# A four-layer graph network: two transposes per graph moved from TensorE to a round trip through HBM, and a new order of the work

## Chip, core and metric

One core of a Trainium2 chip runs the whole program in one launch. The metric is the device time of one execution in microseconds (us), as the median of several runs.

## What is computed

Sixteen graphs of 1024 nodes each have features x (1024 x 128) and a weighted symmetric-pattern adjacency matrix adj (1024 x 1024), all in 32-bit floats. Four layers follow one another, each of the form x = x + layer(relu(layernorm(x))):

```
# layer 0, three times (i = 0, 1, 2), relu between
h = h @ W_i + b_i;  nh = h / |h|
h = (adj * (nh @ nh.T)) @ h
# layer 1
y = relu(((1+eps)*h + h.T-aggregate over adj) @ W1 + b1) @ W2 + b2, masked by nodes
# layer 2
h = h @ W;  e = tanh(s1_i + s2_j);  softmax over the edges;  e @ h
# layer 3
h = x @ W.T + b;  e = (h@A) @ h.T, plus its transpose;  softmax where adj > 0
h' = relu((att * adj) @ h);  three gates from x and h';  o * tanh(sigmoid(i*h' + f*x))
```

## The kernel before

The kernel keeps one graph ("batch" in the code, b = 0 to 15) in SBUF while it goes through its layers. A feature matrix of 1024 x 128 is one tile of 128 partitions x 1024 elements: eight blocks of 128 nodes. The adjacency is worked through in eight rows of blocks, j = 0 to 7, and each row in two halves of 512 columns (HALVES).

No order of the work is written out by hand. The functions `layer0` to `layer3` only record operations in a `Plan`: each has an engine, a planned duration, the tiles that it reads and writes, and a function that emits the instructions. `Plan.order` then lists them: among the operations that could start now on an engine it takes the one with the lowest `rank`, and it gives out buffers within limits per kind of tile (`KINDS`: how many in all, and how many for graphs younger than the oldest one). So up to three graphs are in flight (`AHEAD`), and an engine's instructions of different graphs are interleaved. Each engine executes its list strictly in that order. DMAs are nearly all issued from SP's queue, which is in order too: a DMA that waits for its source holds up those behind it.

Before the change, `rank` is a deadline of the graph (one every 59 planned us), less the planned length of what still hangs on the operation, less a number from the table `LEADS`.

What the change touches:

- `layernorm` makes hn: statistics on VectorE (L700, L709, L711), the power -1/2 on GpSimd (L592), then half of the blocks scaled by VectorE (L728) and the other half by ScalarE with the relu in it (L735). `relu` (L756) is a ScalarE instruction for VectorE's half.
- `flipped` transposes a feature matrix on TensorE: eight 128x128 transposes by the identity in two groups of four (L599), each group into one PSUM bank, and two ScalarE evictions of 128x512 (L652), which do the relu where it is wanted. It is used for layer 0's first features (tile hT, from PSUM tile ps_hT), for h in each of layer 0's three steps (hTn), and in layers 2 and 3 (hnT from ps_hnT; h3T).
- `squares` is the other way to a transpose, and before the change nothing calls it. It writes the matrix to an HBM buffer (one DMA of 512 KB), reads it back in four DMAs of 128 KB in pieces of 32 elements, so that every 32x32 square lands in its transposed place, and turns all squares within themselves by one VectorE transpose of 128x1024. A DMA of the same shape is in use elsewhere: `Square.send` sends the blocks above the diagonal (L832, by_hbm<-above, 512 KB) through HBM and reads them back (L843, got<-by_hbm, 4 x 128 KB) for the squares of layers 0 and 3. The adjacency itself is loaded in squares and turned by VectorE (L939, L947).
- `layer0` uses `squares` for hT if the flag "D" is set and b > 1; `layer3` uses it for hnT if the flag "3" is set.
- After layer 2, the last accumulation (L863, acc<-h,e) is divided by its row sums (L1196 to L1204) and added to x (L674); then comes layer 3's layernorm.
- The first TensorE work on hT is `project` (L630, psP<-w,hT); on layer 3's hnT also L630 (psP<-w3e,hnT), and L640 (pg<-hnT,wg).

Of the kernel before, what the change touches and what calls it, by code (L numbers as in the profile page):

```python
# [11 lines left out]
AF = mybir.ActivationFunctionType  # L12
# [3 lines left out]
P = 128  # L16
N = 1024
NB = N // P
D = 128
# [26 lines left out]
class Op:  # L46
    def __init__(self, engine, us, fn, batch, port, lat):
        self.engine, self.us, self.fn, self.batch, self.port, self.lat = engine, us, fn, batch, port, lat
        self.preds, self.succs, self.after = set(), set(), set()
        self.new, self.bufs = [], []  # L50
        self.waits = 0
        self.tail, self.key = 0.0, None
        self.end = None


class Plan:
# [8 lines left out]
    def __init__(self, pools, kinds, deadline, ahead, window, leads):  # L65


        self.pools, self.kinds = pools, kinds
        self.deadline, self.ahead, self.window, self.leads = deadline, ahead, window, leads
        self.psum = {k for k, v in kinds.items() if v[0] == "bank"}  # L70
        self.ops = []
# [38 lines left out]
    def link(self):  # L110
# [23 lines left out]
        for o in reversed(self.ops):  # L134
            o.tail = o.us + max((s.tail + o.lat for s in o.succs), default=0.0)
            lead = self.leads.get(o.key + o.edge, self.leads.get(o.key, 0.0))
            o.rank = (self.deadline(o.batch) - o.tail - lead, o.seq)
# [87 lines left out]
def tile_adj_preln(  # L225
# [40 lines left out]
    FLAGS = set("CabcdkxhyzTGmrHWM")  # L266
# [61 lines left out]
    for load_it in first:  # L328
# [13 lines left out]
        "adjT": ("adjT", 16, 16), "adjL": ("adjL", 5, 5), "x": ("x", 3, 3), "w4": ("big", 9, 11),  # L342
        "chunk": ("big", 10, 4), "above": ("above", 2, 1), "got": ("got", 1, 1), "ps": ("bank", 8, 8),
        "acc": ("bank", 8, 6), "small": ("small", 8, 15), "row": ("row", 3, 2), "hbm": ("hbm", 3, 3),
        "hrow": ("hrow", 1, 2), "mask": ("mask", 5, 5), "dot": ("dot", 8, 6),
    }
    PERIOD, LAST, AHEAD, WINDOW = 59, 47, 2, 0.05

    LEADS = {
        "T DMA raw": 8063, "T PE raw": 0, "T ACT adjT": -100.5, "T DVE su": 407, "x DMA x": -299,  # L350
        "0 DVE st": -1917, "0 DVE mv": 384.5, "0 POOL rstd": -16.5, "0 DVE nb": 0.5, "0 DVE hn": -46.5,
        "0 ACT hn": -776, "0 PE ps": -292, "0 ACT hT": 79, "00 PE psP": 1440, "00 DVE h": -784,
        "00 PE ps": -672.5, "00 ACT hTn": 614, "00 ACT sq": -476, "00 DVE ss": 222.5, "00 POOL rn": 13,
        "00 PE sq": 10.5, "00 ACT above": 37, "00 DVE ew": 444, "00 PE acc0": -2418.5, "00 POOL params": 0,
        "00 DMA params": -366, "00 DVE params": 242, "00 PE params": 0, "00 ACT hT": 294.5, "01 PE psP": 195.5,
        "01 DVE h": 274.5, "01 PE ps": 22.5, "01 ACT hTn": -282.5, "01 ACT sq": -278, "01 DVE ss": -245,
        "01 POOL rn": 168.5, "01 PE sq": -205.5, "01 ACT above": -385.5, "01 DVE ew": 1895,
        "01 PE acc0": -206.5, "01 ACT hT": 248, "02 PE psP": 2916.5, "02 DVE h": 758, "02 PE ps": 31,
        "02 ACT hTn": -1183.5, "02 ACT sq": -620.5, "02 DVE ss": 22, "02 POOL rn": 75, "02 PE sq": 1500.5,
        "02 ACT above": -53, "02 DVE ew": -1, "02 PE acc0": -128.5, "02 DVE x": -282.5, "T DMA adjT": 69,  # L360
        "T DVE adjT": -537, "1 DVE st": -155, "1 DVE mv": 935.5, "1 POOL rstd": 141.5, "1 DVE nb": 917.5,
        "1 DVE hn": 519, "1 ACT hn": 0, "1 DVE x": 1302, "1 DMA adjL": -249, "1 DVE adjL": -959.5,
        "1 PE acc1": 121, "1 ACT g": -58.5, "1 PE py": -1925.5, "1 ACT y1": -654, "1 PE py2": -657.5,
        "2 DVE st": 2939, "2 DVE mv": 451.5, "2 POOL rstd": -7.5, "2 DVE nb": 458.5, "2 DVE hn": 103.5,
        "2 ACT hn": -1908.5, "2 PE ps": 207, "2 ACT hnT": -1905, "2 DVE alone": 776.5, "2 DVE x": -134,
        "2 PE psP": -2328.5, "2 ACT h": -84.5, "2 DVE hrow": -74, "2 PE pf": -2468, "2 ACT hfl": -232,
        "2 PE pt": -2412, "2 ACT sr": -23.5, "2 DMA sd": 272, "2 DMA s1": -44.5, "2 DVE h": 238.5,
        "2 ACT e2": -712, "2 DVE e2": 1.5, "2 PE acc2": -14.5, "2 DVE rden": -158.5, "3 DVE st": -169,
        "3 DVE mv": 49.5, "3 POOL rstd": -377.5, "3 DVE nb": -198, "3 DVE hn": -200.5, "3 ACT hn": -305,
        "3 PE ps": 733, "3 ACT hnT": 328.5, "3 PE pg": 105, "3 ACT gT": -285, "3 PE psP": 1188.5,  # L370
        "3 DVE h": -34.5, "3 ACT h3T": 171.5, "3 ACT mask": -341, "3 PE sq": 363.5, "3 ACT above": 296,
        "3 DVE e3": -798.5, "3 DVE top": -299.5, "3 ACT e3": 670.5, "3 DVE sum": -391, "3 ACT hs": 802,
        "3 PE acc3": -717, "3 ACT hpT": 0, "3 PE psN": 255.5, "3 ACT hp": 229, "3 DVE gate": -304.5,
        "3 ACT gate": 367.5, "3 POOL z": -81, "3 DVE z": -1115, "3 ACT z": -461, "3 DMA z": -361,
        "00 DVE above": -24.5, "00 DMA by": -55, "00 DMA got": 222, "01 DVE above": -5, "01 DMA by": 71,
        "01 DMA got": -599.5, "02 DVE above": 13, "02 DMA by": 225.5, "02 DMA got": 175, "3 DVE above": -234,
        "3 DMA by": 492, "3 DMA got": -1024.5, "3 DVE mask": -757, "3 POOL e3": 15, "3 POOL hp": -384.5,
        "2 PE p1": -264, "2 ACT s1": 222.5, "T DMA raw <0": -410.5, "T PE raw <0": -234,
        "T ACT adjT <0": -47.5, "T DVE su <0": 695, "x DMA x <0": -310.5, "0 DVE st <0": 245.5,
        "0 DVE mv <0": -814.5, "0 POOL rstd <0": -699, "0 DVE nb <0": 4.5, "0 DVE hn <0": -97.5,  # L380
        "0 ACT hn <0": -48, "0 PE ps <0": 50.5, "0 ACT hT <0": 14, "00 PE psP <0": 107, "00 DVE h <0": -116,
        "00 PE ps <0": -292, "00 ACT hTn <0": 127.5, "00 ACT sq <0": -40, "00 DVE ss <0": 80.5,
        "00 POOL rn <0": 581, "00 PE sq <0": -14, "00 ACT above <0": 604, "00 DVE ew <0": -578,
        "00 PE acc0 <0": -283, "00 POOL params <0": -577, "00 DMA params <0": -90.5, "00 DVE params <0": -71,
        "00 PE params <0": 27, "00 ACT hT <0": -242.5, "01 PE psP <0": 141.5, "01 DVE h <0": -33,
        "01 PE ps <0": -283, "01 ACT hTn <0": -13, "01 ACT sq <0": -152.5, "01 DVE ss <0": 216.5,
        "01 POOL rn <0": 15, "01 PE sq <0": 910.5, "01 ACT above <0": -520.5, "01 DVE ew <0": 130,
        "01 PE acc0 <0": 29, "01 ACT hT <0": -137, "02 PE psP <0": -86, "02 DVE h <0": 136,
        "02 PE ps <0": -146, "02 ACT hTn <0": -22.5, "02 ACT sq <0": 335, "02 DVE ss <0": -136.5,
        "02 POOL rn <0": 159.5, "02 PE sq <0": -157, "02 ACT above <0": 703, "02 DVE ew <0": 157,  # L390
        "02 PE acc0 <0": -197.5, "02 DVE x <0": -109, "T DMA adjT <1": 0, "T DVE adjT <1": -784.5,
        "T ACT adjT <1": 115, "1 DVE st <0": -232, "1 DVE mv <0": -95, "1 POOL rstd <0": -224,
        "1 DVE nb <0": -381.5, "1 DVE hn <0": 457.5, "1 ACT hn <0": 107.5, "1 DVE x <0": 63.5,
        "1 DMA adjL <0": -1413.5, "1 DVE adjL <0": -39, "1 PE acc1 <0": -15.5, "1 ACT g <0": 1108,
        "1 PE py <0": -156.5, "1 ACT y1 <0": 317.5, "1 PE py2 <0": -101, "2 DVE st <0": -262.5,
        "2 DVE mv <0": -681.5, "2 POOL rstd <0": -18, "2 DVE nb <0": 115.5, "2 DVE hn <0": -192,
        "2 ACT hn <0": 439, "2 PE ps <0": 115.5, "2 ACT hnT <0": -20.5, "2 DVE alone <0": 130,
        "2 DVE x <0": 88.5, "2 PE psP <0": 210, "2 ACT h <0": -87.5, "2 DVE hrow <0": -270, "2 PE pf <0": 410,
        "2 ACT hfl <0": -958, "2 PE pt <0": 89.5, "2 ACT sr <0": -58, "2 DMA sd <0": -787, "2 DMA s1 <0": -107,
        "2 DVE h <0": -143.5, "2 ACT e2 <0": 40, "2 DVE e2 <0": -511, "2 PE acc2 <0": 12.5,  # L400
        "2 DVE rden <0": -46.5, "3 DVE st <0": -67.5, "3 DVE mv <0": 182, "3 POOL rstd <0": 198.5,
# [96 lines left out]
    def op(engine, us, reads, writes, fn, port=False, lat=None):  # L498
        o = plan.op(engine, us, reads, writes, fn, now[0], port, lat)
        t = (list(writes) + list(reads))[0]  # L500
        o.key = f"{now[1]} {engine} {(t[0] if isinstance(t, tuple) else t).name.split('_')[0]}"

        o.edge = f" <{now[0]}" if now[0] < 2 else f" >{B - 1 - now[0]}" if now[0] > B - 3 else ""
        return o

    def pe(us, reads, writes, fn):
# [1039 lines left out]
```

## Time and profile before

| | |
|---|---|
| median of 3 runs | 2411.78 us (2411.68 to 2414.8) |
| the profiled execution | 2413.47 us, of which span 2411.7 us |
| mean granted TensorE clock | 0.996 |
| TensorE matmuls busy | 2384.0 us (99%), 11905 records |
| VectorE, ScalarE, GpSimd busy | 1985.5 (82%), 1474.7 (61%), 251.1 (10%) us |
| DMA | 271.31 MB, mean 112 GB/s |

How to read it: the span is from the first to the last instruction of the profiled execution. A matmul of 32-bit floats stands as two records in the trace, a transpose as one. Matmuls overlap in the pipeline, so a record's duration (275 ns for 128 columns) is longer than its cost; what one costs is the distance between the starts of neighbours that wait for nothing. "L852" is line 852 of the kernel. A line of a timeline has: start in us, length in us, engine, line, operation, out<-in, shapes, how many instructions were merged (x), and in brackets the idle time before them with what ended it.

### The profile page before, as it was taken

To read this page: it belongs to the slowest core of one execution; us is meant where nothing else is said; L and a number is where in the kernel's file an instruction comes from. 1 tells how busy PE (TensorE), PEld (TensorE's weight loads), DVE (VectorE), ACT (ScalarE), POOL (GpSimd) and SP (SyncE) were. 2 spreads that over 40 slices of the span, in tenths; PEclk is the share of its full clock that TensorE was granted. 3 is DMA by queue.
4 is the path that set the end of the run, shared out by engine and by line. 5 is a ranking of instruction groups with operands and counts; after the bars stand their busy time and mean duration, and the time that the engine had idled before them with its cause. 6 is when DMAs were issued, how large, how long until landed. Compare 5 with 4: busy or idle time off the path is not lost.

```text
span 2411.7 us, 35199 instructions
## 1 busy us (share of the span) xinstructions
PE 2384.0 (99%) x11905; PEld 1586.1 (66%) x11905; DVE 1985.5 (82%) x5529; ACT 1474.7 (61%) x2629; POOL 251.1 (10%) x168
## 2 busy tenths in 40 slices
PE   8999999999999999999999999999999999999988
PEld 5568576675766757576675766757667575765864
DVE  7658889887888988889888898878898787787767
ACT  7326756656675666666656566565756656654566
POOL 3100010110101010000100101101011100100012
PEclk9999999999999999999999999999999999999998
DMA  9232829457393683928748295573936738045100
GB/s 201 61 105 62 166 63 172 125 105 166 72 176 94 136 152 81 183 62 159 148 86 160 71 171 127 105 160 75 172 102 129 155 76 157 27 76 101 34 11 18
DMA packets 1103541, 271.31 MB, mean 112 GB/s; under 512 B 937224, under 2 KB 1084816, under 8 KB 1103360
## 3 DMA queue, kind: packets, MB, share of 16 engines
q1 hardware_dynamic: 1083200, 258.35, 53.7%
q10 hardware_dynamic: 19264, 9.70, 1.4%
q8 instruction: 94, 1.54, 0.3%
q0 software_dynamic: 896, 1.01, 0.2%
q14 instruction: 87, 0.71, 0.1%
HBM read 206.00 MB, written 62.98 MB: 112 GB/s over the span
## 4 chain that ended last, share of the span: by engine, by line
PE 95%; SPq 1%; DVE 1%; ACT 1%; DMA 1%; issue 0%; DVEq 0%
PE acc L852 35%; PE sq L790 20%; PE acc L863 18%; PE psP L630 6%; PE sq L800 4%; PE py L1081 2%; PE py L640 2%; PE ps_hTn L599 2%; PE psN L630 1%; PE ps_hnT L599 1%; PE pg L640 1%; SPq L939 1%; PE ps_h3T L599 1%; PE ps_hT L599 0%; ACT e L1175 0%; DVE ew L1019 0%
## 5 line engine op out<-in xcount | busy, mean ns | idle before, releaser
L1019 DVE SCALAR_TENSOR_TENSOR ew<-sq,rn,adjT 128x512 f32<-128x512 f32 x612 | 434.4, 739 | 86.8 <-ACT above L822 53.6
L852 PE MATMUL acc<-ew,h 128*128 128x512 f32 x1024 | 478.1, 593 | 1.5 <-DVE ew L1019 1.5
L790 PE MATMUL sq<-hTn 128*128 128x512 f32 (+3 forms) x1152 | 432.2, 489 | 0.1
L822 ACT COPY above<-sq 128x384 f32<-128x384 f32 (+3 forms) x432 | 167.7, 393 | 415.9 <-PE sq L800 225.1
L790 PEld LDWEIGHTS sq<-hTn 128*128 128x128 f32 x1152 | 196.9, 190 | 148.3 <-issue 95.7
L852 PEld LDWEIGHTS acc<-ew,h 128*128 128x128 f32 x1024 | 180.4, 190 | 166.2 <-issue 137.3
L863 PEld LDWEIGHTS acc<-h,ew 128*128 128x128 f32 x2048 | 241.0, 192 | 19.9 <-issue 11.4
L863 PE MATMUL acc<-h,ew 128*128 128x128 f32 x2048 | 249.6, 275 | 0.0
L852 PE MATMUL acc<-e,hs 128*128 128x512 f32 x512 | 238.3, 594 | 0.0
L863 PEld LDWEIGHTS acc<-h,e 128*128 128x128 f32 x2048 | 231.8, 192 | 8.4 <-PE acc L852 3.5
L863 PE MATMUL acc<-h,e 128*128 128x129 f32 x2048 | 233.3, 275 | 0.1
L852 PE MATMUL acc<-adjL,hn 128*128 128x512 f32 x512 | 232.8, 592 | 0.0
L592 POOL TENSOR_TENSOR rstd<-ve,mhalf 128x8 f32<-128x8 f32 x64 | 108.9, 1702 | 1054.4 <-DVE ve L711 989.1
L800 PEld LDWEIGHTS sq<-ident,above 128*128 128x128 f32 x960 | 126.1, 141 | 113.1 <-issue 89.7
L950 ACT ACTIVATE adjT<-adjT 128x1024 f32<-128x1024 f32 x120 | 126.6, 1055 | 101.0 <-DVE adjT L947 99.2
L800 PE MATMUL sq<-ident,above 128*128 128x128 f32 x960 | 175.2, 273 | 0.0
L1183 DVE SCALAR_TENSOR_TENSOR e<-adjT,e 128x512 f32<-128x512 f32 x256 | 159.6, 682 | 11.9 <-ACT e L1179 11.9
L1313 DVE TENSOR_TENSOR e<-e,adjT 128x512 f32<-128x512 f32 x248 | 162.0, 682 | 3.8 <-ACT e L1304 3.7
L852 PEld LDWEIGHTS acc<-adjL,hn 128*128 128x128 f32 x512 | 93.5, 190 | 101.2 <-issue 87.7
L812 DVE STREAM_TRANSPOSE above<-sq 128x512 f32<-128x512 f32 x208 | 145.0, 706 | 15.8 <-PE sq L790 14.7
L947 DVE STREAM_TRANSPOSE adjT<-adjT 128x1024 f32<-128x1024 f32 x120 | 144.5, 1221 | 13.9 <-DMA adjT<-in_adj_dram 13.2
L1272 DVE CUSTOM_DVE_ANT_0 e<-mask,sq 128x512 f32<-128x512 int8 x204 | 135.5, 676 | 20.1 <-ACT above L822 12.0
(161 smaller groups left out, 3672.2 us busy)
## 6 DMA issues: line engine op xcount, KB each, us to landing
adjL<-in_adj_dram SPq DMA_DIRECT2D x128, 512.0 KB, 5.0
adjT<-in_adj_dram SPq DMA_DIRECT2D x480, 128.0 KB, 3.9
by_hbm<-above SPq DMA_DIRECT2D x104, 512.0 KB, 4.0
got<-by_hbm SPq DMA_DIRECT2D x416, 128.0 KB, 3.0
s<-sd SPq DMA_DIRECT2D x15, 512.0 KB, 3.5
out_dram<-z ACTq DMA_DIRECT2D x15, 512.0 KB, 3.3
x<-in_x_dram SPq DMA_DIRECT2D x13, 512.0 KB
raw<-in_adj_dram SPq DMA_DIRECT2D x8, 512.0 KB, 8.0
```

Of the source, the lines that this page charges most:

```text
L630: nc.tensor.matmul(dst.t[:, (c - lo) * n : (c - lo + 1) * n], cols(srcT.t, c), w, start=True, stop=True)
L790: lambda: nc.tensor.matmul(dst.t[:, (first - lo) * P :], cols(leftT.t, j), span(rightT.t, first, hi), start=True, stop=True),
L800: nc.tensor.transpose(cols(dst.t, r), cols(above.t, p), ident)
L812: lambda: nc.vector.transpose(span(above.t, p, p + 4), read.t),
L822: lambda: nc.scalar.copy(span(above.t, p, p + hi - first), read.t[:, (first - lo) * P :]),
L852: lambda s=s, lo=lo, hi=hi: nc.tensor.matmul(acc[s].t, cols(h.t, at, w), span(ew.t, lo, hi), start=(j == 0), stop=(j == NB - 1)),
L863: nc.tensor.matmul(a.t[:, (c - lo) * n : (c - lo + 1) * n], cols(ew.t, c), h.t[:, at * w : at * w + n], start=(j == 0 and c == lo), stop=( ...
L947: dve(V(N), [t], [t], lambda t=t: nc.vector.transpose(t.t, t.t), True)
L1019: lambda view=view, ew=ew, rn=rn, j=j, lo=lo, hi=hi: nc.vector.scalar_tensor_tensor(by_block(span(ew.t, lo, hi), D, 4), view(), rn.t[:, j ...
L1183: lambda e=e, j=j, lo=lo, hi=hi: nc.vector.scalar_tensor_tensor(span(e.t, lo, hi), span(aT[j].t, lo, hi), 0.0, span(e.t, lo, hi), op0=ALU. ...
L1272: lambda e=e, view=view, mask=mask, peak=peak, s=s, lo=lo, hi=hi: nc.vector.tensor_tensor_reduce(by_block(span(e.t, lo, hi), D, 4), by_blo ...
L1313: lambda e=e, j=j, lo=lo, hi=hi: nc.vector.tensor_mul(span(e.t, lo, hi), span(e.t, lo, hi), span(aT[j].t, lo, hi)),
```

## The change

Four things:

1. The flags "D" and "3" are set, so `squares` takes the place of `flipped` for layer 0's first features in graphs 2 to 15 (14 graphs) and, with an added condition 0 < b < 14, for layer 3's hn in graphs 1 to 13 (13 graphs). `squares` gets a width parameter, used only in code behind flags that are not set ("4", "6").
2. `rank` is now the time at which the operation is due: graph number times PERIOD plus an entry of the table TIMES, which has one number for each single operation of a kind (LEADS had one for all of a kind). Tables for the first two and the last two graphs stand apart, as they did.
3. PERIOD is 144.89 in place of 59. It is a number of the planner.
4. The limits in KINDS change for most kinds; the pools themselves are as before.

```diff
-            o.rank = (self.deadline(o.batch) - o.tail - lead, o.seq)
...
-    FLAGS = set("CabcdkxhyzTGmrHWM")
+    FLAGS = set("CabcdkxhyzTGmrHWMD3")
...
-        ... "w4": ("big", 9, 11),
-        "chunk": ("big", 10, 4), "above": ("above", 2, 1), ... "ps": ("bank", 8, 8),
-        "acc": ("bank", 8, 6), "small": ("small", 8, 15), "row": ("row", 3, 2), "hbm": ("hbm", 3, 3),
-        "hrow": ("hrow", 1, 2), "mask": ("mask", 5, 5), "dot": ("dot", 8, 6),
+        ... "w4": ("big", 9, 6),
+        "chunk": ("big", 9, 8), "above": ("above", 2, 2), ... "ps": ("bank", 6, 7),
+        "acc": ("bank", 6, 8), "small": ("small", 9, 12), "row": ("row", 2, 4), "hbm": ("hbm", 3, 2),
+        "hrow": ("hrow", 2, 1), "mask": ("mask", 5, 5), "dot": ("dot", 10, 8),
...
-    PERIOD, LAST, AHEAD, WINDOW = 59, 47, 2, 0.05
+    PERIOD, AHEAD, WINDOW = 144.89, 2, 0.05
...
+    TIMES = {
+        "T DMA raw <0": [45.7, -38, -16.15, 49.25, 9.05, 10.9, 32.75, 4.4],
...
+        o.nth = counts.get((o.batch, o.key), 0)
+        counts[o.batch, o.key] = o.nth + 1
+        due = TIMES[o.key + o.edge if o.key + o.edge in TIMES else o.key][o.nth]
+        o.rank = (o.batch * PERIOD + due, o.seq)
...
-        if "3" in FLAGS and b < B - 2:
+        if "3" in FLAGS and 0 < b < B - 2:
             relu(hn)
             hnT = squares(hn, f"hnT_{k}")
         else:
             hnT = flipped(hn, f"hnT_{k}", AF.Relu)
             relu(hn)
```

The function that takes the place of `flipped`, as it stands before (the change only adds a width to the read):

```
    def squares(src, name):
        d = Buf("hbm", [N, D], f"d_{name}")
        op("DMA", 0.7, [src], [d], lambda: nc.sync.dma_start(..., by_block(src.t)), lat=2.2)
        dst = w4(name)
        def fetch():
            v = d.t.rearrange("(a i) (g j) -> g i a j", i=SQ, j=SQ)
            for g in range(P // SQ):
                nc.sync.dma_start(dst.t[g * SQ : (g + 1) * SQ, 0:N].rearrange(...), v[g])
        op("DMA", 3.6, [d], [dst], fetch, lat=2.4)
        dve(V(N), [dst], [dst], lambda: nc.vector.transpose(dst.t[:, 0:N], dst.t[:, 0:N]), True)
        return dst
```

In the built program this is, against before: 216 TensorE transposes fewer; 27 VectorE transposes of 128x1024 more; 54 ScalarE evictions of 128x512 fewer and 14 relus of 128x512 more; 27 writes of 512 KB and 108 reads of 128 KB more on SP's queue. Everything else is there in the same number (some are merged or split by four or eight blocks), in another order.

## Prediction

> **What bounds the kernel now.** I read the page's busy line first, then stretches of one graph each, then the stretch between layer 2 and layer 3 of one graph on TensorE, and last the end of the span.
>
> ```profile
> PE 2384.0 (99%) x11905; PEld 1586.1 (66%) x11905; DVE 1985.5 (82%) x5529; ACT 1474.7 (61%) x2629; POOL 251.1 (10%) x168
> ```
>
> A busy TensorE alone proves little, so I take the distance between starts. Each group's usual distance (429 ns for a record of 512 columns, 112 ns for 128, 109 ns for a transpose), times its records, sums to 2361.6 us. The first matmul starts at 7.6 and the last group ends at 2400.9, so some 32 us in all lie in longer distances; 10.8 us follow the last matmul. The kernel is bound by how much TensorE is given to do.
>
> The stretches of busy time, here two of four periods that I read (us, then busy us of PE, PEld, DVE, ACT, POOL; granted clock; DMA share; GB/s):
>
> ```profile
> 904.10:1050.70 146.60, 146.60 (x728) 97.08 (x727) 125.46 (x349) 92.33 (x163) 13.70 (x8) 1.00 0.63 126
> 1050.70:1197.30 146.60, 146.60 (x728) 97.09 (x727) 125.46 (x349) 92.34 (x163) 13.70 (x8) 1.00 0.64 126
> ```
>
> They repeat to the digit. One graph's records at the usual distances come to 145.75 us, so only 0.87 us of a period is waiting. VectorE has 21 us free in each, ScalarE 54.
>
> TensorE's timeline between layer 2's last product of one graph and its layer 3:
>
> ```profile
> 1065.73 1.17 PE L863 MATMUL acc<-h,e 128*128 128x129 f32 x9
> ...
> 1077.28 0.60 PE L599 MATMUL ps_hT<-ident,hn 128*128 128x128 f32 x4
> 1077.72 2.84 PE L630 MATMUL psP<-w,hT 128*128 128x128 f32 x24
> 1080.40 1.04 PE L599 MATMUL ps_hnT<-ident,hn 128*128 128x128 f32 x8
> 1081.27 1.04 PE L599 MATMUL ps_hTn<-ident,h 128*128 128x128 f32 x8
> ```
>
> Layer 2 ends at 1066.90; the transposes of layer 3's hn start 13.5 us later and take 0.87 us for eight (1080.40 to 1081.27), 109 ns each. ScalarE's timeline says when hn was ready:
>
> ```profile
> 1078.46 1.64 ACT L735 ACTIVATE hn<-x,nb,rstd 128x128 f32<-128x128 f32 x4
> ```
>
> At 1080.10, 13.2 us after layer 2: hn comes just in time. That chain stays, and it decides whether a longer route to the transposed hn fits.
>
> [...]
> - [...] a transpose's record is 273 ns long, its cost 109 ns.
> - [...] The trace has VectorE's turn of 128x1024 at 1221 ns (L947), TensorE's eight at 0.87 us plus two evictions of 0.593.
> [...]
>
> **The change part by part.**
>
> *TensorE gives up 216 transposes* (8 for each of 14 layer-0 and 13 layer-3 turns): 216 x 0.109 = 23.6 us. All of it lies on the bounding engine. In the middle, 16 x 0.109 = 1.74 us per period.
>
> *ScalarE* gives up 54 evictions (L652, 0.595) and gains 14 relus (L756, 0.62): -23.5 us of an engine with 54 us free per period; nothing on the path.
>
> *VectorE* gains 27 x 1.22 = 33 us, two turns a period: 125.5 + 2.4 of then 144.9 us, 88%. Hidden behind TensorE's matmuls while 17 us a period are free; without that cover 33 us.
>
> *DMA:* 27 writes and 108 reads, 28 MB, on SP's queue, which moved 258 MB. Share 0.64 to about 0.70. By itself hidden.
>
> *The new waits.* The route for layer 3 is hn, relu of VectorE's half, write, read, VectorE's turn. Its time I take from the like-shaped DMAs of `Square.send`, SP's timeline:
>
> ```profile
> 1044.44 0.37 SPq L832 DMA_DIRECT2D by_hbm<-above  x1
> 1047.45 2.26 SPq L843 DMA_DIRECT2D got<-by_hbm  x4
> ```
>
> The write releases the first read after 3.0 us; the last read is issued some 4.6 us after the write and lands 2.2 to 3.3 us later by that tile's view: about 7.5 us in all. Among other traffic it is longer: 1090.39 to 1093.78 and 3.14 us of issuing, plus the median 3.0 to landing, 9.5; the page's median 4.0 for the write makes it 10.1. In the stretch that matters, before, DMA rests:
>
> ```profile
> 1080.40:1090.30 9.90, 9.90 (x59) 7.19 (x58) 6.97 (x16) 6.59 (x13) 1.64 (x1) 1.00 0.00 1
> ```
>
> and in the built order SP has nothing between layer 0's read and this write. So I take 7.5, upper end 10.1. From layer 2's end: 13.2 + 0.6 relu + 0.2 issue + 7.5 + 1.2 turn + 0.2 = 22.9 us. In the built order of the changed kernel, TensorE has between graph 7's last layer-2 product and its first use of hnT 14 matmuls of 512 columns (0.858), 2 of 384, 2 of 256, 30 of 128 and 28 transposes: 23.9 us, where before it was 13.7 to the transposes. Margin 1.0 us, so no stall; at 10.1, 1.6 us late. Queued behind VectorE's waiting turn are layer 0's multiplications (ew, L1019) of the next graph, and TensorE's accumulations wait for those.
>
> Layer 0's route starts from x, loaded long ahead; the write goes out before layer 3's in SP's order and its turn stands on VectorE between nb and other work, so only DMA time above some 10 us would show. Cost 0; upper end 1 us a turn.
>
> *The new order elsewhere.* 0.87 us of waiting per period may go or double: -10 to +10 us over 12 periods; I take 0. At the start the same transposes of the raw adjacency stand first; the transition through graphs 1 to 3 is new: +2, range -1 to +5.
>
> *The end.* TensorE's timeline and the stretch there:
>
> ```profile
> 2344.26 1.88 PE L852 MATMUL acc<-e,hs 128*128 128x512 f32 x4
> 2350.80 1.22 PE L790 MATMUL sq<-h3T,gT 128*128 128x256 f32 x2 [4.66 <-DVE peak L1272]
> ```
> ```profile
> 2341.05:2353.31 12.26, 7.60 (x36) 5.17 (x33) 12.19 (x49) 4.64 (x11) 4.31 (x3) 0.84 0.00 1
> 2353.31:2382.60 29.29, 28.60 (x95) 15.99 (x95) 24.94 (x71) 21.13 (x43) 4.73 (x2) 0.89 0.00 1
> ```
>
> Graph 15's layer 2 ends at 2341.05, its layer-3 transposes start 12.26 us later with 6.3 us of work between, and the idle 4.66 us bring a reduced clock (0.84, 0.89). By the usual distances, 50.0 us of work take 59.8 (2341.05 to 2400.9): 9.8 lost. In the new order 8.7 us of graph 14's layer 3 stand in the gap, and VectorE has no other graph's work inside the chain (before: two masks, three e, 3.3 us, of which about half only filled GpSimd's 1.7 us), so the chain is about 10.8 and the idle 2.1 us, below the 4.66 that cost the clock. But graph 14 then ends before graph 15's layer 3 begins: its 31.6 us of matmuls run with nothing to fill waits. VectorE needs about 3.1 us per row of blocks there, TensorE as much; I allow 5 us of waits (0 to 12). Loss 7.1 against 9.8: -2.7, from -9 to +5. The 10.8 us after the last matmul stay: the same operations.
>
> **Sum.** -23.6 - 2.7 + 2 = -24.3. The profiled execution: 2413.5 - 24.3 = 2389.2, span 2387.4. The median shown is 1.7 below the profiled one: 2411.8 - 24.3 = 2387.5 us.
>
> **Rivals.**
> - *Layer 3's turn comes late.* At 9.5 to 10.1 us of DMA the turn is 1.0 to 1.6 us late, times 13: 13 to 21 us of the gain lost, about 2404. For it: a margin of only 1 us on a chain just in time. Against: the quiet stretch.
> - *Slower: the late turn holds VectorE.* The same wait with its queue: every us that the read of hnT is late, VectorE stands, then ew, then TensorE. It turns the sign when 13 turns lose more than 24.3 us, 1.9 us each; slower by over 0.2% (4.8 us) from 2.2 us, a round trip of 10.7. At 3 us each: 2387.5 + 39 = 2427. Against: only if traffic falls there.
> - *More than the transposes.* The order also removes most of the 0.87 us per period and the reduced clock: 2387.5 - 8 = 2379.
> - *The planner's order doesn't hold on the chip:* VectorE at 88% leaves short waits everywhere, 1.7 us a period, so 14 periods eat the gain: within 0.2%, 2411.
>
> **How the numbers follow.** Within 0.2% (2407 to 2416.6) is about what a measurement can tell from no change. Forecast (2382 to 2394) 0.58; late turns (2394 to 2407) 0.19; more (below 2382) 0.13; no change 0.05; slower 0.05. Faster 0.90. The range 2379 to 2404 leaves about 0.2 out and holds the DMA bounds up to 1.3 us a turn.
>
> **What would show it.** Right: TensorE records 216 fewer; a period of 144.9 us; DVE 127.9 busy in it; psP<-w3e,hnT without idle time before it; no reduced clock before the last 12 us. Wrong: psP or pg waiting for the turn of hnT in every graph (late turns), ew waiting on DMA, a period near 146.6, or a gap above 4 us at the end.

## The result and the profile after

The changed kernel takes 2389.4 us (median of 5 runs, 2387.22 to 2391.87), beside 2414.8 us for the kernel before on the same chip (5 runs, 2411.68 to 2415.37): a ratio of 0.990, interval 0.9885 to 0.9914. A second set of runs (below) gave 2388.54 us and 0.9897 (0.9884 to 0.9911). The forecast was 2387.5, the range 2379 to 2404. The profiled execution took 2391.87 us, with a span of 2390.1; it is the slowest of the five.

The page's busy line:

```profile
PE 2355.8 (99%) x11689; PEld 1565.0 (65%) x11689; DVE 2023.5 (85%) x5556; ACT 1454.3 (61%) x2589; POOL 247.2 (10%) x168
```

TensorE has 216 records fewer, VectorE is busy for 38 us longer. Two periods in the middle (us; busy us of PE, PEld, DVE, ACT, POOL; granted clock; DMA share; GB/s):

```profile
919.72:1064.00 144.28, 144.23 (x713) 95.60 (x712) 128.35 (x350) 90.68 (x159) 13.32 (x8) 1.00 0.73 143
1064.00:1208.29 144.29, 144.24 (x713) 95.62 (x712) 128.35 (x350) 90.69 (x159) 13.32 (x8) 1.00 0.71 143
```

A period fell from 146.6 to 144.28 us. By the usual distances its work is 144.01 us, 1.74 less than before; the wait in it is 0.27 instead of 0.87. Layer 3's turn of one graph, whose layer 2 ends at 1064.00, on SP's queue, VectorE and TensorE:

```profile
1077.73 0.38 SPq L1173 DMA_DIRECT2D d_hnT<-hn  x1
1081.10 2.35 SPq L1181 DMA_DIRECT2D hnT<-d_hnT  x4
```
```profile
1085.30 1.37 DVE L1584 SCALAR_TENSOR_TENSOR ew<-sq,rn,adjT 128x512 f32<-128x512 f32 x2
1086.59 1.24 DVE L1186 STREAM_TRANSPOSE hnT<-hnT 128x1024 f32<-128x1024 f32 x1
1087.75 0.71 DVE L1584 SCALAR_TENSOR_TENSOR ew<-sq,rn,adjT 128x512 f32<-128x512 f32 x1
```
```profile
1083.81 1.95 PE L1428 MATMUL acc<-h,ew 128*128 128x128 f32 x16
...
1087.22 1.06 PE L1428 MATMUL acc<-h,ew 128*128 128x128 f32 x8
1088.11 1.95 PE L1195 MATMUL psP<-w3e,hnT 128*128 128x131 f32 x16
```

The write goes out at 1077.73, 13.73 us after layer 2; the turn ends at 1087.83; TensorE comes to psP<-w3e,hnT at 1088.11 and has no idle time before it. Room is left, but only 0.3 us. VectorE comes to the turn straight from ew, without idle time, in 12 of the 13 graphs, this one included: its own list holds the turn until then too.

At the start and the end the trace is less smooth. Where TensorE's starts lie further apart than usual, I count the difference as waiting (the excess, by start distances). It sums to 33.5 us against 31.5 before: 16.4 against 8.1 in the first 450 us, 3.4 against 9.8 in the middle (450 to 1950), 1.8 against 0 up to 2250, 11.8 against 13.5 after that. So the spans differ by -23.6 + 2.0 = -21.6 us (2411.7 to 2390.1). The medians of the two kernels differ by 25.4 us, and a second profile of the changed kernel (experiment 9, below), with less waiting at the start and the end, has a span of 2386.2, 25.5 below before. The transposes' 23.6 us are the same in both profiles; the waiting moves by some 4 us.

### The profile page after: what moved, and what is told of

Its sections match the earlier page's. It is cut to its first block, busy times and chain, and to the rows that moved or that the text cites. A ratio compares the mean times of both kernels' runs of the same rounds, so it can differ in the third digit from the quotient of the medians.

```text
span 2390.1 us, 35188 instructions
## 1 busy us (share of the span) xinstructions
PE 2355.8 (99%) x11689; PEld 1565.0 (65%) x11689; DVE 2023.5 (85%) x5556; ACT 1454.3 (61%) x2589; POOL 247.2 (10%) x168
## 4 chain that ended last, share of the span: by engine, by line
PE 93%; DVE 3%; ACT 2%; DMA 1%; SPq 1%; issue 0%; DVEq 0%; ACTq 0%
PE acc L1417 36%; PE sq L1355 20%; PE acc L1428 18%; PE psP L1195 5%; PE sq L1365 4%; PE py L1646 2%; PE py L1205 2%; PE ps_hTn L1164 1%; PE pg L1205 1%; PE psN L1195 1%; SPq L1504 1%; PE ps_h3T L1164 1%; DVE h L1239 1%; PE ps_hnT L1164 1%; DVE ew L1584 0%; DVE x L1239 0%
## 5 line engine op out<-in xcount | busy, mean ns | idle before, releaser
L1417 PE MATMUL acc<-e,hs 128*128 128x512 f32 x512 | 246.1, 597 | 2.9 <-DVE e L1890 2.9
L1890 DVE TENSOR_TENSOR e<-e,adjT 128x512 f32<-128x512 f32 x248 | 163.9, 682 | 11.3 <-ACT e L1881 11.1
L1417 PEld LDWEIGHTS acc<-adjL,hn 128*128 128x128 f32 x512 | 94.8, 190 | 107.5 <-issue 92.9
L1838 ACT ACTIVATE mask<-adjT 128x1024 int8<-128x1024 f32 x112 | 117.9, 1054 | 59.2 <-DVE peak L1849 59.0
```

Source lines behind the costliest of these rows:

```text
L1417: lambda s=s, lo=lo, hi=hi: nc.tensor.matmul(acc[s].t, cols(h.t, at, w), span(ew.t, lo, hi), start=(j == 0), stop=(j == NB - 1)),
L1890: lambda e=e, j=j, lo=lo, hi=hi: nc.vector.tensor_mul(span(e.t, lo, hi), span(e.t, lo, hi), span(aT[j].t, lo, hi)),
```

## The experiments

My theory: the 24 us are TensorE's transposes and nothing else, and the new order is what makes room for the route. The rival: the gain comes from the new order. A second question was how near layer 3's route is to costing something. The experiments are numbered in the order in which they ran (what was expected of one refers to earlier ones), and told by question.

### The transposes put back into the new order

`plan.order()` runs as in the changed kernel; then write, read and turn of 26 of the 27 routes are dropped from the list (graph 15's for layer 0 stays), and the transposes and evictions are put in where hn is ready and a PSUM bank is free.

```diff
+    drop.update((put, get, turn))
...
-        for o in ordered:
+        for i, o in enumerate(ordered):
+            for src, dst, slot in insert.get(i, ()):
+                for s, (lo, hi) in enumerate(HALVES):
+                    p = psum.tile([P, HALF], F32, tag=f"bank_{slot}", ...)
+                    for c in range(lo, hi):
+                        nc.tensor.transpose(cols(p, c - lo), cols(src.t, c), ident)
+                    nc.scalar.activation(span(dst.t, lo, hi), span(p, 0, hi - lo), AF.Copy)
+            if o in drop:
+                continue
```

Experiment 1:

> The changed kernel's order, but the turns of layer 3 (13 graphs) and of layer 0 (graphs 2 to 14) stand on TensorE again, each put into the same list of work where hn is ready; graph 15's layer 0 keeps the new route. Theory (the gain is TensorE's transposes and nothing else): 26 x 8 x 0.109 = 22.7 us more than the changed kernel, 2389.4 + 22.7 = 2412 us, a period of 144.3 + 1.74 = 146.0 us. Rival (the new order gives the gain, the transposes would fit into waits): below 2395 us.

Measured: 2440.18 us, 1.0109 of before (1.0094 to 1.0124). Neither number. TensorE's waits (total us, times, longest) between 600 and 2000 us say why:

```profile
PE ps_hnT L2131 <- ACT hnT L2132: 6.9, 10, 0.7
PE ps_hT L2131 <- ACT hT L2132: 6.9, 10, 0.7
```

Both groups of four used one bank, so the second waited for the first one's eviction, in every turn: a wait that my placing made. Experiment 5 gives them two banks, or puts the second 1.6 us later:

```diff
-            for src, dst, slot in insert.get(i, ()):
-                for s, (lo, hi) in enumerate(HALVES):
+            for src, dst, slot, s in insert.get(i, ()):
+                lo, hi = HALVES[s]
```

> As the first of these experiments, but each turn's two groups of four transposes go to two PSUM banks (or 1.6 us apart), so that the second group doesn't wait for the first one's eviction. Theory (the first experiment's 51 us were 22.7 us of transposes and waits for evictions, 0.7 us twice per graph, that its own placing made): 2389.4 + 22.7 = 2412 us, up to 2416 where single waits stay; TensorE's waits for hT and hnT evictions gone. Rival (the new order itself can't take the transposes): again above 2425 us.

Measured: 2412.45 us, 0.9997 of before (0.9989 to 1.0006). That is 23.05 us more than the changed kernel for 208 transposes that should cost 22.7, and those waits are gone. The new order without the new route is worth nothing that can be told from no change. The rival falls. (The new order is ranks and buffer limits together; no run tells these apart.)

### The route put into the old order

In the kernel before, write and reads follow hn as early as the list allows, and VectorE's turn stands ahead of the first use.

```diff
+        drop.update(four)
+        insert.setdefault(ordered[first], []).append((0, n))
+        insert.setdefault(ordered[use], []).append((1, n))
...
+            for step, n in insert.get(o, ()):
+                if step == 0:
+                    put(src, dst, hbm.tile([N, D], F32, tag=f"turn_{n % 2}", ...))
+                else:
+                    nc.vector.transpose(dst.t[:, 0:N], dst.t[:, 0:N])
```

`put` emits the relu, the write and the four reads; `four` are the two transposes and evictions dropped.

Experiment 2, both routes:

> The order of before, but the turns of layer 3 (13 graphs) and of layer 0 (graphs 3 to 15) go by the new route, written as soon as hn is ready, turned just before their first use. Theory (the new order is needed to make room for the route): hnT is ready 10.6 us after hn (the changed kernel's trace), but TensorE comes to its first use 1.2 us after hn: 9.4 us late, 13 x 9.4 = 122 us, less 22.7 us of transposes: 2414.8 + 99 = 2514 us, with psP<-w3e,hnT waiting some 9 us in each of 13 graphs. Rival (any order will do, other graphs' work covers it): 2414.8 - 22.7 = 2392 us.

Measured: 2556.23 us, 1.0588 of before (1.0572 to 1.0603). The rival, that any order will do, falls. The theory's waits are there (13 waits for hnT with 94.8 us of idle time in the trace), but the loss is 42 us larger; experiment 12 below shows what the theory left out.

Experiment 3, layer 0's route alone:

> The order of before, with layer 0's turn alone by the new route (graphs 3 to 15); layer 3 stays on TensorE. Theory (layer 0's route needs no new order, since hn lies ready some 14 us before its use): 13 x 8 x 0.109 = 11.3 us less, 2414.8 - 11.3 = 2403.5 us. Rival (the turn holds VectorE inside layer 2's chain, or the write holds SP's queue): no gain, 2415 us or more.

Measured: 2433.9 us, 1.0079 (1.0062 to 1.0096): slower, as the rival said, but not by its mechanism: it is the turn itself that comes late. VectorE's and TensorE's timelines show where:

```profile
1086.99 0.17 DVE L726 SCALAR_TENSOR_TENSOR nb<-mv,rstd 128x8 f32<-128x8 f32 x1 [1.81 <-POOL rstd L592]
1087.08 1.11 DVE L735 TENSOR_SCALAR hn<-x,mv,rstd 128x128 f32<-128x128 f32 x4
1088.11 1.12 DVE L681 SCALAR_TENSOR_TENSOR h<-psP,rn,b 128x128 f32<-128x128 f32 x4
1089.14 1.23 DVE L1543 STREAM_TRANSPOSE hT<-hT 128x1024 f32<-128x1024 f32 x1
```
```profile
1090.47 1.13 PE L630 MATMUL psP<-w,hT 128*128 128x128 f32 x8 [1.53 <-issue]
```

VectorE has no idle time before the turn, so it did not wait for the data; the turn stood behind nb, hn and h in VectorE's list, and TensorE needed it 1.5 us sooner. Ahead of nb VectorE waits 1.81 us for GpSimd: a hole that holds the whole turn. Experiment 6 puts it there:

```diff
-        insert.setdefault(ordered[use], []).append((1, n))
+        turn = ordered[use] if late else next(
+            (o for o in ordered if o.key == "3 DVE nb" and o.batch == four[0].batch - 2 and at[o] < use),
+            next(o for o in ordered if o.at > ordered[use].at - 3),
+        )
+        insert.setdefault(turn, []).append((1, n))
```

> As the third of these experiments (order of before, layer 0's route in graphs 3 to 15), but VectorE's turn stands ahead of layer 3's nb of the graph before last, where VectorE waits 1.81 us for GpSimd's rstd, and no longer behind hn. Theory (the route is free, only the turn's place in VectorE's list cost 1.5 us per graph): 2414.8 - 11.3 = 2403.5 us and no wait of psP<-w,hT. Rival (the write in SP's queue or the relu on ScalarE cost the rest): above 2410 us.

Measured: 2406.76 us, 0.9971 (0.996 to 0.9983), 7.5 us less than before; theory 11.3. The period's waiting is 0.97 us against 0.88 before, so the route is free where it repeats; the trace has 2.4 us more waiting in the first 150 us, 1.2 more from 300 to 450 and 1.3 more around graph 15. VectorE's timeline has the turn in the hole:

```profile
1075.12 0.17 DVE L718 TENSOR_SCALAR ve<-mv 128x8 f32<-128x8 f32 x1
1075.30 1.25 DVE L1547 STREAM_TRANSPOSE hT<-hT 128x1024 f32<-128x1024 f32 x1
1077.11 0.17 DVE L726 SCALAR_TENSOR_TENSOR nb<-mv,rstd 128x8 f32<-128x8 f32 x1 [0.56 <-POOL rstd L592]
```

Experiment 12, both routes and this early turn:

> As the second of these experiments (the order of before with both routes), but layer 0's turns stand early on VectorE. Theory (the second experiment's 141 us were 13 waits for hnT of 7.3 us, 13 waits for layer 0's turn of 1.7 us, some 4 us of half clock after each long wait, less 22.7 us of transposes): without the 22 us of layer 0's waits 95 + 52 - 22.7 = 124 us more than before, 2538 us. Rival (the loss comes from somewhere else): 2550 us or more.

Measured: 2550.72 us, 1.0574 (1.0559 to 1.0588). That is the rival's number, and the theory's is 13 us off, though the loss still comes from hnT. By the distance to before on its own chip it is 3.9 us less than with the late turn (137.7 against 141.6), not 18: I had added up waits that overlap. While TensorE waited 1.7 us for layer 0's turn, hnT was already under way; without that wait TensorE comes to hnT sooner and waits there longer, by the start distances 9.2 us instead of 7.5. TensorE's waits over the span, VectorE, TensorE, and the stretches around one such wait:

```profile
PE psP L630 <- DVE hnT L1547: 117.5, 13, 9.8
```
```profile
1139.73 1.25 DVE L1547 STREAM_TRANSPOSE hnT<-hnT 128x1024 f32<-128x1024 f32 x1 [7.09 <-DMA hnT<-d_hnT]
```
```profile
1130.73 1.04 PE L599 MATMUL ps_hTn<-ident,h 128*128 128x128 f32 x8
1141.03 3.86 PE L630 MATMUL psP<-w3e,hnT 128*128 128x131 f32 x16 [9.27 <-DVE hnT L1547]
1144.68 2.71 PE L640 MATMUL pg<-hnT,wg 128*128 128x512 f32 x4
```
```profile
1131.00:1141.00 10.00, 0.76 (x7) 0.53 (x5) 2.83 (x5) 2.55 (x5) 0.00 (x0) 0.76 0.61 105
1141.00:1146.00 5.00, 4.97 (x18) 4.33 (x19) 2.73 (x6) 0.00 (x0) 0.63 (x1) 0.50 0.00 0
```

The wait is the 9.4 us that I had worked out for experiment 2. What I left out is in the last line: for 5 us after the wait TensorE has half its clock, so the 16 matmuls of psP take 3.86 us instead of 1.95 (the changed kernel's line above). The period is 157.0 us (the waits begin at 974.7, 1131.6 and 1288.7); without waits for hnT it would be 146.6 - 1.74 = 144.9. So 12.1 us a turn, of which 9.2 are waiting and the rest is the clock: 13 x 12.1 - 22.7 = 135 us, and 138 were measured. The old order with these routes loses 5.7%; the new order, worth nothing by itself, is their condition. (Layer 3's route alone in the old order was not run; that the loss is its own follows from experiment 6, where layer 0's route alone gains.)

### How much room layer 3's route has

Experiment 4: layer 3's reads wait for one more small read of the same buffer (a hop).

```diff
+            if name.startswith("hnT"):
+                nc.sync.dma_start(dst.t[0:1, 0:SQ], d.t[0:1, 0:SQ])
             for g in range(P // SQ):
```

> The changed kernel, but layer 3's four reads wait for one more small read (32 numbers) of what was written: the route is longer by one trip, about 2 us by the 2.4 to 3.0 us from issue to landing of hT's reads. Theory (the margin of layer 3's turn is used up, 0.3 us): 13 x (2.0 - 0.3) = 22 us more, 2411 us, psP<-w3e,hnT waiting 1.7 us in 13 graphs. With the predicted margin of 1.0 us: 13 us more, 2402. Rival (the wait is not on the path, since TensorE's work behind makes up for it): 2389 to 2391 us.

Measured: 2406.97 us, 0.9965 of before (0.9953 to 0.9977), 17.6 more than the changed kernel. SP's queue and TensorE in one period:

```profile
1085.73 0.38 SPq L1173 DMA_DIRECT2D d_hnT<-hn  x1
1089.24 0.23 SPq L1180 DMA_DIRECT2D hnT<-d_hnT  x1
1090.66 2.33 SPq L1183 DMA_DIRECT2D hnT<-d_hnT  x4
```
```profile
1097.69 2.05 PE L1197 MATMUL psP<-w3e,hnT 128*128 128x131 f32 x16 [1.42 <-DVE hnT L1188]
```

Here the four reads follow the write after 4.93 us instead of 3.37, 1.56 later. This graph is one of the late ones: over the 13 graphs the median is 4.48 us against 3.28, and VectorE's turn starts 1.3 us later on average, not the 2.0 that I took from landing times. Less the room of 0.3 that is 1.0 late, 13 us in all; with room of 1.0 it would be 4. By start distances TensorE's waits for hnT sum to 14.8 us, and one of them, of 2.30 us, was followed by 3.41 us of half clock, 1.7 us more. The room is the measured one.

Experiment 11, two such reads, one after the other:

> The changed kernel, with two small reads, one after the other, ahead of layer 3's four reads: the route is longer by twice the 1.55 us that one cost, so 13 turns are 2.8 us late. One hop cost 17.6 us. Theory [...]: 13 x 2.8 = 37, and 11 to 22 us of half clock, so 2437 to 2448 us, with a mean clock of 0.98 to 0.985. Rival (only the wait counts): 2389.4 + 37 = 2426 us at most, with the clock at 0.997.

Measured: 2422.43 us, 33.9 more than the changed kernel beside it (next part) and slower than before: 1.0039 (1.0026 to 1.0053). That is the rival's number. The 37 us in both forecasts were too high, since 1.55 us was the hop of a late graph: two hops start the turn 2.3 us later on average. By start distances the 13 waits sum to 27.6 us, and the trace's span is 28.2 to 32.1 us longer than in the changed kernel's two profiles. TensorE's waits between 300 and 2200 us:

```profile
PE psP L1198 <- DVE hnT L1189: 22.6, 11, 3.3
PE pg L1208 <- DVE hnT L1189: 1.7, 1, 1.7
PE psP L1198 <- issue: 1.1, 1, 1.1
```

None of these 13 waits (1.3 to 3.5 us by start distances) was followed by half clock, which I had expected after every other one; the mean granted clock of the profiled execution is 0.997, as in the changed kernel's. That was my estimate, and what tells the waits with half clock from these 13, the runs do not show.

### VectorE's cover, and the start

Experiment 8 leaves VectorE's turns out:

```diff
-        dve(V(N), [dst], [dst], lambda: nc.vector.transpose(dst.t[:, 0:N], dst.t[:, 0:N]), True)
+        dve(V(N), [dst], [dst], lambda: None, True)
```

> The changed kernel with the 27 VectorE turns left out (the squares land in their places, but stay unturned within themselves). Theory (VectorE's 33 us lie beside TensorE's work, only the end of layer 3's route is 1.24 us earlier): 0 to 4 us less, 2386 to 2389 us. Rival (VectorE at 89% costs some waiting everywhere): 10 to 33 us less.

Measured: 2389.35 us, 0.9899 of before (0.9884 to 0.9914). The stretches of the same two periods:

```profile
919.72:1064.00 144.28, 144.23 (x712) 95.54 (x711) 126.35 (x349) 90.69 (x159) 13.32 (x8) 1.00 0.72 143
1064.00:1208.29 144.29, 144.24 (x712) 95.53 (x711) 126.33 (x349) 90.67 (x159) 13.32 (x8) 1.00 0.71 142
```

VectorE is busy 2.0 us less a period and the period is the same to the hundredth. VectorE's 33 us are hidden whole, at 89% busy.

The start loses 8 us more than before; two waits of TensorE in the first 450 us go back to VectorE waiting in its list for a DMA (TensorE's waits, then VectorE's timeline):

```profile
PE ps_hTn L1164 <- DVE h L1542: 2.6, 1, 2.6
PE acc L1417 <- DVE ew L1584: 2.5, 2, 2.3
```
```profile
38.35 1.25 DVE L1512 STREAM_TRANSPOSE adjT<-adjT 128x1024 f32<-128x1024 f32 x1 [2.59 <-DMA adjT<-in_adj_dram]
68.71 1.41 DVE L1584 SCALAR_TENSOR_TENSOR ew<-got,rn,adjT 128x512 f32<-128x512 f32 x2 [6.64 <-DMA got<-by_hbm]
```

So VectorE's adjacency turns of graph 1 were moved 3 us later in its list, and one load behind the reads of got on SP's (experiment 7):

```diff
+    for o in [o for o in ordered if o.key == "T DVE adjT" and o.batch == 1 and o.at < 48]:
+        later(o, 3.0)
+    ordered.remove(load)
+    ordered.insert(ordered.index(last) + 1, load)
```

> The changed kernel, but at the start VectorE takes graph 1's adjacency turns 3 us later in its list, and SP takes graph 0's first load for layer 1 behind graph 1's reads of got. Theory (the start lost 5 us more than before to TensorE waiting on VectorE, which waited on DMA: 2.6 us at 38 us and 2.3 us at 67 us, the latter followed by 3.4 us of half clock, 1.7 us): 2.5 + 2 + 1.7 = 6 us less, 2383.5 us, and no half clock before 2350 us. Rival (DMA is the bound of the start, so the wait only moves): 2388 to 2390 us.

Measured: 2387.75 us, 0.9893 (0.9879 to 0.9906). As this is within the spread, both kernels ran once more on one chip (experiments 9 and 10):

> The changed kernel once more, beside the start experiment on the same chip: 2389.4 us by its first runs. It is the measure for the next run.

> The start experiment once more. Its first runs gave 2387.75 us, 1.65 less than the changed kernel's, within the spread of both. Theory (one wait of 2.6 us at 38 us is gone, and the half clock more often than not): 1.5 to 3 us below the changed kernel on the same chip, so the better version by less than 0.15%. Rival (the start is bound by DMA, so nothing stays of it): the same within 0.5 us.

Measured: 2388.54 us for the changed kernel (0.9897, 0.9884 to 0.9911) and 2388.71 for the other (0.9896, 0.9883 to 0.991). Nothing stays. The 2.6 us wait is gone in the trace of the edited one, but TensorE still waits 1.9 us for ew, and ew 6.3 us for got, and the changed kernel's own start varies by as much between its profiles (10.6 and 8.3 us of excess in the first 150 us). No version that I ran beats the changed kernel by more than the spread.

## Why the prediction was right, point by point

- *216 transposes, -23.6 us.* Right. TensorE's work by the usual distances went from 2361.6 to 2338.0 us, and putting 208 of them back cost 23.05 us (22.7 by the same price).
- *ScalarE, VectorE, DMA hidden.* Right. VectorE shown by leaving the turns out (0 us); ScalarE and DMA (share 0.71 to 0.73, forecast 0.70) only argued: TensorE doesn't wait for them in the repeated period.
- *Layer 3's turn, 22.9 us against 23.9.* The mechanism was right, a term mis-sized. hn came at +13.2, as worked out, and the write at +13.73 (worked out: 14.0). The DMA part is 8.7 us where I took 7.5 (bounds 7.5 to 10.1): 3.3 to the first read instead of 3.0, 4.9 to 5.2 to the last one's issue instead of 4.6, and 3.5 to its landing instead of 2.2 to 3.3. And a step was missing: VectorE's list has ew ahead of the turn, so that the turn starts 8.85 us or more after the write even in the graph whose last read landed after 7.75. In this order, reads as short as I took would hardly have left more room. First use is at +24.1. The room was 0.3 us, not 1.0; there was no stall, but by that little (TensorE waited for hnT once, 0.5 us in graph 1).
- *Layer 0's route, 0.* Right in the period (0.1 us in experiment 6), but the reason that I gave was only half of it: the turn must not stand behind nb, hn and h. There it made TensorE wait 1.7 us in each graph (experiment 3, by start distances); in VectorE's 1.8 us wait for GpSimd it is free.
- *Waiting per period, 0; start and transition, +2.* Both sizes off, with opposite signs: the period's wait fell by 0.6 (6.4 us in the middle), the first 450 us lost 8.3 more (5.5 in the second profile), above my +5. They nearly cancel, which is luck in the sum.
- *The end, -2.7.* Near: the loss after graph 15's layer 2 is 5.8 us against 9.8 (4.1 in the second profile), where I had 7.1. But not as told: before psP<-w3e,hnT TensorE idles 0.64 us only, the larger gap (2.4 us) is in layer 3, and 3.7 us of gaps are in layer 2 just before, so from 2250 us on only 1.7 us are gained (3.5 in the second profile). "Below the 4.66 that cost the clock" was wrong as a criterion: half clock followed the 2.4 us gap as well. So the sign "no reduced clock before the last 12 us" failed, with 3.41 us of half clock at 2363.5 and, after a wait of 2.3 us, at 69.7.
- *The slower rival* was priced rightly: it said that the sign turns at 1.9 us a turn. With two hops the loss is 33.9 / 13 = 2.6 us a turn, and the kernel is slower than before; with one hop (17.6 / 13 = 1.4) it is still faster. So the change of sign was some 2 us of DMA time away, the first loss only 0.3. Its mechanism was not the one seen: TensorE waited for hnT itself, not for ew behind it.
- *More than the transposes:* a part of its mechanism came, 0.6 of the 0.87 us of waiting a period, but the start took it back. *Late turns* and *no change:* not seen.

## What to carry to other kernels

On an engine that is 99% busy, price a change by start distances: eight transposes of 109 ns are worth 0.87 us whatever their records say. Work given to an engine with 15 us free per period cost nothing where nothing waited behind it (experiment 8), and 1.7 us a graph at a wrong place in the list of one with 21 us free (experiment 3). A longer route is free only if the order puts enough other work ahead of its first use: the same routes (all but one) were worth -25 us in one order and +138 in the other, and each us beyond the room is paid once per graph. Place the waiting instruction in a hole that its engine has anyway (a turn of 1.25 us in a wait of 1.81, experiment 6), and don't add up waits along one in-order engine: take one away, and the next grows (from 7.5 to 9.2 us in experiment 12).

## What the runs showed of the hardware

Some of TensorE's waits were followed by half clock, and others of like length were not:

- Before: 4.66 us idle ahead of sq<-h3T,gT at 2350.80; the clock is 0.50 from 2350 to 2354 and from 2354 to 2358.
- The changed kernel, first profile: 2.32 us idle ahead of acc<-ew,h at 69.51, then 3.41 us of half clock from 69.7 on; 2.22 us idle (2.38 by start distances) ahead of acc<-e,hs at 2362.70, then 3.41 us of it from 2363.5 on.
- The changed kernel, second profile (experiment 9): the same gap at the end, and no half clock after it. The mean granted clock is 0.998 there, 0.997 in the first.
- One hop (experiment 4): a wait of 2.30 us, then 3.41 us of half clock.
- Two hops (experiment 11): 13 waits of up to 3.47 us by start distances, and no half clock after any of them. After 2.27 us idle the 16 matmuls of psP took 2.05 us.
- Both routes in the old order (experiment 12): 9.27 us idle, then 0.50 from 1141 to 1146; the 16 matmuls of psP took 3.86 us.

The end of the first profile of the changed kernel, in stretches of busy time (the clock third from the end):

```profile
2357.00:2363.00 6.00, 3.78 (x16) 2.14 (x15) 5.94 (x18) 5.58 (x12) 4.26 (x2) 1.00 0.00 1
2363.00:2367.00 4.00, 4.00 (x6) 1.54 (x5) 4.00 (x13) 2.99 (x7) 0.00 (x0) 0.57 0.41 130
```

So the length of a gap did not decide by itself: half clock followed 2.30 us in one run and not 3.47 us in another, and the same 2.38 us in one execution of a kernel and not in the next. What else decides, these runs do not show.
